# Attention's products in reverse order, a layer's weights through a ring of five buffers, and a bias added by an accumulating DMA

## The chip, the cores and the metric

The kernel runs on one core of a Trainium2 chip. A core has a matrix engine (TensorE, PE), a vector engine (VectorE, DVE), an activation engine (ScalarE, ACT), a general engine (GpSimd, POOL) and an engine that mostly issues transfers (SyncE, SP). Each of them executes its own list of instructions in the order in which it is written, and waits on semaphores for the others. Transfers run on 16 DMA engines, which serve several queues. In this kernel POOL issues the gathers (indirect DMAs) and some plain DMAs, all on one software queue, and SP issues most of the rest.

The metric is device time in microseconds (us) of one execution.

## The reference, cut to what matters

Two layers with the same outline, x = x + gnn(norm(x)) and then x = x + ffn(norm(x)), over x of 32 samples x 512 tokens x 256 features, with one adjacency matrix (512x512) for each sample.

Layer 0's ffn, for each token:

```python
t = max over d of (x[d] + Wt[f, d]) + bt[f]      # for each of 1024 features f
trop = s * max_i(t*sl_cvx + of_cvx) + (1-s) * min_i(t*sl_ccv + of_ccv)
classical = gelu(x @ Wc + bc);  g = sigmoid(x @ Wg + bg)
out = (g * trop + (1 - g) * classical) @ Wd + bd
```

`bd`, 256 numbers, is layer 0's last bias. Layer 1's gnn is attention with 4 heads of width 64 over the adjacency:

```python
h = einsum('bnd,hde->bhne', x, W)
weight = leaky_relu(e_src[i] + e_dst[j]), where adj == 0: -1e9
dst = einsum('bhij,bhje->bhie', softmax(weight), h) + bias
out = layernorm(relu(dst) + h) * gamma + beta
```

Layer 1's ffn assigns every token softly to 64 slices for each of 8 heads (`W_x`, `b_x`, `W_slice`, `b_slice`), gathers slice tokens (`W_fx`), runs a two-way state space scan with gates over the 64 slice tokens (`hy_in_w` of 1168x512, `hy_fcD_w` of 8x512, `hy_out_w` of 512x512), spreads the result back to the tokens and multiplies by `out_w` (256x512).

## The kernel before, in words

All is in float32. P is 128, the number of partitions; N is 512, the tokens of a sample; NT is 4, the tiles of 128 tokens in it; D is 256.

**Layer 0** (`layer0_sorted`). The gnn part (`convs`) goes over the samples in segments, normalises, and sorts the tokens of a segment by how many candidates their maximum over d needs. It writes a row for each token into a table in DRAM, `rows_of`, with its values and the indices of its largest entries. The ffn (`feed_forwards`) then works on 32 groups of 512 sorted tokens. Of a group:

- `sums` gathers the tokens' rows into `xs` (L553, four gathers of 128 rows on POOL), normalises each tile on ACT (`xn`, L574) and transposes it on PE. For each tile it gathers the table row of the largest entry (`best`, L564) and, one by one, those of the further entries (`rows`, L595); DVE takes the maximum into `best` (L598), after ACT added the value of the entry to its first row (L592). At its end come four adds on POOL, one for each tile, of the constant `bd` to `xs` (L610). `bd` is loaded at the start into all 128 partitions (L135 is the line of the helper that does it).
- `mixed` does the products with Wc and Wg (`clsp`, `gatep`, L623), transposes `best` (`tz`, L630), bends it (ACT L632 and L636, DVE L637) and blends (`acc`, up to L641).
- `down` multiplies by Wd (`po`, L652), adds into `xs` on DVE (L654), and stores `xs` to `x2s` in DRAM by a DMA of SP (L655).

`mixed` of a group is woven with `sums` of the next one; `down` of the group before comes after the first step of `mixed`. So the add of `bd` to a group's `xs` is written a whole group ahead of that group's `down`.

**The generator `ahead`**. Alongside, `feed_forwards` is woven with a second stream of steps, `ahead`: the convolutions of the later segments, and after these the beginning of layer 1 (`layer1_plain`). This beginning loads and transposes layer 1's weights, so their loading falls into layer 0's late groups, near 1850 to 2000 us. `load_T` (L995 to L1011) takes a weight in pieces of 128 rows: SP loads a piece into a buffer of the pool `raw` (L1005), PE transposes its blocks of 128 columns (L1009), ACT copies the result (L1010), and a step of the generator ends. W_fx has 4 pieces of 128x256, hy_in_w 9 of 128x512 and one of 16x512, hy_out_w 4, out_w 2 and hy_fcD_w one of 8x512: 21 in all. There are two buffers for each width of a piece. After them comes the block that forms the product of W_x and W_slice (`wsl`, up to L1075); it loads W_slice, W_x, b_x and b_slice itself, and squares `wsl` into a buffer `wsl2` (L1066).

**Layer 1** (`layer1_plain`). For each sample `prepare` gathers x, adds `ln_beta` by an accumulating DMA of POOL from a DRAM tile that holds the row four times (`add_rows`, L949), and makes the values `hv` and the terms of the weights. `attention` then goes over the four tiles j of 128 source tokens. Of each tile, DVE makes four weights `att`, one for each head, 128x512 each (L1220), in the order of the heads, some turns ahead; there are 13 buffers for them. When the last two heads' turn is there, PE makes all of the tile's products:

- eight `avp` products (L1256): two for each head, each with 32 columns of `hv` and the whole 128x512 weight. The output of the k-th goes to partitions 32k to 32k+31 of one of two PSUM tiles. So the four products of a PSUM tile use the four different groups of 32 columns of the array.
- four `adp` products (L1261), one for each head, for the sums that divide: again one for each column group.

The products of a tile are written in the order of the heads, so the first one takes the weight that was made first. The ffn (`mixer`) of two samples at a time is interleaved with the attention of later samples by a credit scheme. Its products are `lgp` L1342, `yTp` L1354, `xp` L1407, `gp` L1494, `segp` L1498, `xtp` L1503, `qp` L1508, `yp` L1524, `oTp` L1542, `outp` L1574; `hp` L1187 and `x3T` L1149 are of `prepare` of the next sample.

**Order**. The lines above are written by Python generators, and a scheduler then sets the order of each engine's list from what depends on what. The engines execute that list as it stands: an instruction that waits holds back what stands behind it on its engine.

Of the kernel before, what the change touches and what calls it, by code (L numbers as in the profile page):

```python
# [19 lines left out]
P = 128  # L20
# [77 lines left out]
def layer0_sorted(tc, ident, eps, x, adj, w, x2s, ranks, over, following):  # L98
# [29 lines left out]
    with ExitStack() as ctx:  # L128
# [9 lines left out]
        w_msg = const("w_msg", [P, DC, D], w["W_msg"].rearrange("(c p) u -> p c u", p=P))  # L138
        w_upd = const("w_upd", [P, DC, D], w["W_upd"].rearrange("(c p) u -> p c u", p=P))
        bias = const("bias", [P, D], w["bias"].partition_broadcast(P))  # L140
        bd = const("bd", [P, D], w["bd"].partition_broadcast(P))
        wc = cst.tile([P, DC, FFN], F32, tag="wc", name="wc")
        wg = cst.tile([P, DC, FFN], F32, tag="wg", name="wg")
        wd = cst.tile([P, FC, D], F32, tag="wd", name="wd")
# [398 lines left out]
        def feed_forwards():  # L543


            def sums(s, g):
# [57 lines left out]
                for c in range(DC):  # L604
# [1 line left out]
                nc.vector.tensor_tensor(over[:, s * ST : (s + 1) * ST].rearrange("p (t g) -> p g t", g=NG)[:, g, :],  # L606
                                        xg[:, :, COUNT], limits.rearrange("p (t g) -> p g t", g=NG)[:, g, :],
                                        ALU.is_gt)
                for t in range(NT):
                    nc.gpsimd.tensor_add(xg[:, t, :D], xg[:, t, :D], bd)  # L610
                got[s, g] = xg, xnT, best

            def mixed(s, g):
# [251 lines left out]
def layer1_plain(tc, ident, eps, x2s, ranks, adj, w, out, over, ps):  # L865
# [35 lines left out]
    with ExitStack() as ctx:  # L901
# [94 lines left out]

        with tc.tile_pool(name="raw", bufs=2, side="right") as raw:

            def load_T(dst, src, name):

                R, Ccols = src.shape
                for r0 in range(0, R, P):
                    n = min(P, R - r0)
                    t = raw.tile([P, Ccols], F32, tag=f"raw{Ccols}", name=f"{name}_{r0}")
                    nc.sync.dma_start(t[:n], src[r0 : r0 + n, :])  # L1005
                    pt = psum("tp", f"{name}p{r0}").rearrange("p (c r) -> p c r", r=P)
                    cs = Ccols // P
                    for c in range(cs):
                        nc.tensor.transpose(pt[:, c, :n], t[:n, c * P : (c + 1) * P], ident[:n, :n])  # L1009
                    nc.scalar.copy(dst[:, :, r0 : r0 + n], pt[:, :cs, :n])  # L1010
                    yield  # L1011

            yield from load_T(wfxT, w["W_fx"], "wfx")
            yield from load_T(inT, w["hy_in_w"], "in")
            yield from load_T(hoT, w["hy_out_w"], "ho")
            yield from load_T(owT, w["out_w"], "ow")
            yield from load_T(fcT, w["hy_fcD_w"], "fc")
# [5 lines left out]
            def twice_T(src, name):  # L1023

                R, Ccols = src.shape
                t = raw.tile([P, 2, Ccols], F32, tag="twice", name=name)
                for i in range(2):
                    nc.sync.dma_start(t[:R, i, :], src)
                pt = psum("tp", f"{name}p")
                nc.tensor.transpose(pt[:, :R], t[:R].rearrange("p i c -> p (i c)"), ident[:R, :R])  # L1030
                return pt


            wsT = raw.tile([P, G], F32, tag="wsT", name="wsT")
            nc.vector.tensor_copy(wsT, twice_T(w["W_slice"], "ws")[:, :G])
            wx = raw.tile([P, KC, D], F32, tag="wx", name="wx", bufs=1)
            nc.sync.dma_start(wx, w["W_x"].rearrange("(k p) d -> p k d", p=P))
            bx = raw.tile([P, KC], F32, tag="bx", name="bx")
            nc.sync.dma_start(bx, w["b_x"].rearrange("(k p) -> p k", p=P))
            bsl = raw.tile([1, H, G], F32, tag="bsl", name="bsl", bufs=1)  # L1040
            bs = raw.tile([1, G], F32, tag="bs", name="bs")
            nc.sync.dma_start(bs, w["b_slice"].rearrange("(o n) -> o n", o=1))
            for c in range(DC + 1):
                M = P if c < DC else 1
                for i in range(H // KC):

                    half = slice(i * C, (i + 1) * C)
                    px = psum("mm", f"wslp{c}_{i}")
                    for k in range(KC):
                        lhs = wx[half, k, c * P : (c + 1) * P] if c < DC else bx[half, k : k + 1]  # L1050
                        nc.tensor.matmul(px[:M, k * G : (k + 1) * G], lhs, wsT[half, :], start=True, stop=True)
                    px = px[:M, : KC * G].rearrange("p (k g) -> p k g", k=KC)
                    rt = rtemp[:M, i :: H // KC].unsqueeze(2).to_broadcast([M, KC, G])
                    if c < DC:
# [168 lines left out]
        def attention(b):  # L1223
# [21 lines left out]
            for i, (q, j) in enumerate(turns):  # L1245
# [4 lines left out]

                if q + 1 == AP:
                    ends = dict(start=j == 0, stop=j == NT - 1)
                    for p in range(AP):
                        for k in range(2 * HO // HW):
                            h, e = 2 * p + k * HW // HO, k * HW % HO
                            nc.tensor.matmul(pv[p][k * HW : (k + 1) * HW, :], hv[:, j, h, e : e + HW],  # L1256
                                             weighed[b, h, j], **ends)
                    if j == 0:
                        pd = psum("pv", f"adp{b}")
                    for h in range(AH):  # L1260
                        nc.tensor.matmul(pd[h * HW : (h + 1) * HW, :], hv[:, j, h, HO:].to_broadcast([P, HW]),  # L1261
                                         weighed.pop((b, h, j)), **ends)
                yield
# [983 lines left out]
```

## Time and profile before

| | |
|---|---|
| time, median of three runs | 4365.9 us (4364.42 to 4366.94) |
| profiled execution, its own time | 4372.35 us |
| span of the profiled execution | 4370.6 us |
| mean granted PE clock | 0.955 |
| PE busy | 3882.4 us, 89% |
| DVE busy | 3279.3 us, 75% |
| ACT busy | 2295.0 us, 53% |
| POOL busy | 1617.9 us, 37% |
| DMA, mean over the span | 116 GB/s |

The span is from the first to the last instruction. In the views that follow, a row of a stage names its stretch in us, then for each engine its busy time and its number of instructions; PEclk is the granted share of PE's full clock, and "DMA share" the mean busy share of the 16 DMA engines. A row "L1256 PE MATMUL avp<-att,hv 128*32 128x512 f32" reads: line 1256, on PE, a matmul with output `avp` from `att` and `hv`, with a stationary operand of 128x32 and a moving one of 128x512. In a row of waits, the first name is what stood and the second is what it stood for; the numbers are total us, times, and the longest. The chain of waits is followed backwards from the last instruction, at each step to what released it.

Layer 0's convolutions and groups fill the time up to about 2400 us, and layer 1's samples the time after it.

### The profile page before, as it was taken

The page shows a single profiled execution, that of the slowest core. Times are in us where ns is not written, and L with a number is a line of the kernel's source. Part 1 is how long each engine was busy: PE and PEld are TensorE (multiplying, and loading weights), DVE is VectorE, ACT ScalarE, POOL GpSimd, SP SyncE. Part 2 cuts the span into 40 slices and gives each one's busy share as a digit, 9 for nine tenths or more (in the row PEclk, how much of TensorE's full clock was granted, in tenths as well). Part 3 has the DMA queues.
Part 4 walks back from the last instruction along what each step waited for, and adds up shares of the span by engine and source line. Part 5 has one row for each costly group of instructions (what it writes and reads, how often), then busy time and mean ns, then how long its engine had stood idle before and what let it go on. Part 6 is the DMA issues. An engine that isn't in the chain of part 4 may idle for free.

```text
span 4370.6 us, 57973 instructions
## 1 busy us (share of the span) xinstructions
PE 3882.4 (89%) x20311; PEld 2456.1 (56%) x20311; DVE 3279.3 (75%) x7008; ACT 2295.0 (53%) x4756; POOL 1617.9 (37%) x2036
## 2 busy tenths in 40 slices
PE   5567898988989999888998899999999999999997
PEld 4454565565655666554555455655555555555555
DVE  6668887898878978877775777777777777777763
ACT  3345655566655656546564555555554455554533
POOL 2346644665536644354431322222222222222210
PEclk8778999999999999998999999999999999999998
DMA  5546543564436644375441322222222322222200
GB/s 128 160 154 216 179 156 126 165 218 143 153 117 199 199 156 135 93 250 167 147 133 40 95 73 73 69 65 72 68 68 76 78 75 78 64 74 77 61 25 21
DMA packets 244051, 507.52 MB, mean 116 GB/s; under 512 B 39299, under 2 KB 114827, under 8 KB 243748
## 3 DMA queue, kind: packets, MB, share of 16 engines
q0 software_dynamic: 107904, 349.50, 26.7%
q1 hardware_dynamic: 135844, 154.21, 11.3%
q8 instruction: 162, 2.65, 0.2%
q14 instruction: 141, 1.16, 0.1%
HBM read 446.46 MB, written 57.17 MB: 115 GB/s over the span
## 4 chain that ended last, share of the span: by engine, by line
DVE 33%; PE 32%; DMA 11%; issue 9%; POOL 8%; ACT 5%; SPq 0%; another core or an unknown queue 0%; DVEq 0%; POOLq 0%; ACTq 0%
DVE att L1220 4%; DVE acc L637 4%; PE clsp L623 4%; PE gatep L623 3%; PE po L652 3%; PE avp L1256 3%; DMA rows<-table,xs 2%; DVE best L598 2%; DMA rows<-table,tops 2%; DVE sw L1349 2%; DVE sst L1347 2%; PE yTp L1354 2%; DVE sw L1344 2%; PE oTp L1542 1%; DMA best<-table,xs 1%
## 5 line engine op out<-in xcount | busy, mean ns | idle before, releaser
L623 PE MATMUL clsp<-xnT,wc 128*128 128x512 f32 x1024 | 521.8, 628 | 55.5 <-ACT cls L625 39.7
L623 PE MATMUL gatep<-xnT,wg 128*128 128x512 f32 x1024 | 502.1, 609 | 10.5 <-ACT gate L625 9.7
L652 PE MATMUL po<-wd,acc 128*128 128x256 f32 x2048 | 456.9, 382 | 6.5 <-DVE acc L641 3.5
L652 PEld LDWEIGHTS po<-wd,acc 128*128 128x128 f32 x2048 | 388.8, 191 | 73.1 <-issue 9.2
L1220 DVE SCALAR_TENSOR_TENSOR att<-own,other,mask 128x512 f32<-128x512 f32 x512 | 366.1, 744 | 76.4 <-DMA own<-ownd 76.4
L637 DVE SCALAR_TENSOR_TENSOR acc<-past,fld,acc 128x512 f32<-128x512 f32 x448 | 346.3, 776 | 28.3 <-ACT past L636 20.3
L598 DVE SCALAR_TENSOR_TENSOR best<-rows,xs,best 128x1024 f32<-128x1024 f32 x212 | 273.1, 1290 | 121.4 <-ACT best L592 75.8
L632 ACT ACTIVATE acc<-tz,fld 128x512 f32<-128x512 f32 x256 | 199.0, 778 | 269.1 <-PE tz L630 237.5
L623 PEld LDWEIGHTS gatep<-xnT,wg 128*128 128x128 f32 x1024 | 197.3, 197 | 254.0 <-issue 200.8
L636 ACT ACTIVATE past<-tz,fld 128x512 f32<-128x512 f32 x448 | 291.6, 694 | 73.6 <-DVE acc L637 72.1
L595 POOL DMA_INDIRECT rows<-table,xs x212 | 247.3, 1166 | 176.7 <-DVE best L598 121.8
L1256 PE MATMUL avp<-att,hv 128*32 128x512 f32 x2048 | 297.4, 599 | 6.1 <-DVE att L1220 6.1
L623 PEld LDWEIGHTS clsp<-xnT,wc 128*128 128x128 f32 x1024 | 182.6, 199 | 195.2 <-issue 114.3
L434 PE MATMUL pm<-h,adj 128*128 128x258 f32 (+1 forms) x1024 | 178.9, 321 | 100.3 <-DVE keep L427 34.4
L625 ACT ACTIVATE gate<-gatep,fld 128x512 f32<-128x512 f32 x256 | 175.6, 686 | 153.4 <-PE gatep L623 130.4
L1342 PE MATMUL lgp<-wsl,x4T 128*128 128x512 f32 x512 | 241.4, 610 | 14.3 <-ACT sw L1343 6.7
L1354 PE MATMUL yTp<-sw,x 128*128 128x512 f32 x512 | 237.0, 602 | 17.4 <-DVE sw L1349 16.9
L1161 POOL DMA_INDIRECT x<-x2s,ranks x128 | 135.2, 1056 | 295.5 <-DVE att L1220 147.5
L553 POOL DMA_INDIRECT xs<-rows_of,order x128 | 158.8, 1241 | 229.7 <-DVE acc L637 111.8
L1307 POOL TENSOR_TENSOR mu<-mu,eps 128x16 f32<-128x16 f32 x32 | 111.3, 3478 | 350.4 <-DVE mu L1306 350.4
L1574 PE MATMUL outp<-v,swT 128*128 128x256 f32 x1024 | 227.6, 381 | 0.0
L625 ACT ACTIVATE cls<-clsp,fld 128x512 f32<-128x512 f32 x256 | 176.3, 689 | 94.4 <-PE clsp L623 59.1
(598 smaller groups left out, 8809.0 us busy)
## 6 DMA issues: line engine op xcount, KB each, us to landing
adj<-in_adj POOLq DMA_DIRECT2D x128, 256.0 KB
ai<-in_adj SPq DMA_DIRECT2D x128, 256.0 KB
x<-added POOLq DMA_DIRECT2D x64, 512.0 KB
own<-ownd SPq DMA_DIRECT2D x128, 256.0 KB
rows_of<-keep SPq DMA_DIRECT2D x32, 550.0 KB
x<-in_x SPq DMA_DIRECT2D x32, 512.0 KB
x2s<-xs SPq DMA_DIRECT2D x32, 512.0 KB
out<-x SPq DMA_DIRECT2D x32, 512.0 KB
```

Source lines behind the costliest of these rows:

```text
L595: nc.gpsimd.indirect_dma_start(out=row, out_offset=None, in_=table, in_offset=bass.IndirectOffsetOnAxis(ap=idxs[:, k : k + 1].bitcast(U32) ...
L598: nc.vector.scalar_tensor_tensor(m, row, vals[:, k : k + 1], m, ALU.add, ALU.max)
L623: nc.tensor.matmul(pf, wf[:, c, f * P : (f + 1) * P], xnT[:, c, :], start=c == 0, stop=c == DC - 1)
L625: nc.scalar.activation(o, pf, fn, bias=fld[:, f, bf : bf + 1], scale=1.0 if fn == AF.Gelu else 0.5)
L636: nc.scalar.activation(r, z, AF.Relu, bias=fld[:, f, AT + b : AT + b + 1])
L637: nc.vector.scalar_tensor_tensor(y, r, fld[:, f, CH + b : CH + b + 1], y, ALU.mult, ALU.add)
L652: nc.tensor.matmul(po[:, i, :], acc[f][:, t * P : (t + 1) * P], wd[:, f, :], start=f == 0, stop=f == FC - 1)
L1220: nc.vector.scalar_tensor_tensor(e, own[h], other[:, j, h : h + 1], mask[:, j, :], ALU.max, ALU.mult)
L1256: nc.tensor.matmul(pv[p][k * HW : (k + 1) * HW, :], hv[:, j, h, e : e + HW], weighed[b, h, j], **ends)
L1342: nc.tensor.matmul(pf, xnT[:, c, t * P : (t + 1) * P], wsl[:, c, :], start=c == 0, stop=c == DC - 1)
L1354: nc.tensor.matmul(py, xn[:, t, c * P : (c + 1) * P], sw[:, t, :], start=t == 0, stop=t == NT - 1)
L1574: nc.tensor.matmul(po[:, :D], swT[:, k, t * P : (t + 1) * P], v[:, k, :], start=k == 0, stop=k == KC - 1)
```

## The change

Three edits.

1. **`bd` by an accumulating DMA.** The constant in 128 partitions and its load go. A DRAM tile of four rows is filled with the 256 numbers four times. For each group, in the place of the four adds on POOL, one DMA issued by POOL adds this tile, broadcast to all partitions, to the first 256 columns of the four rows of `xs` in each partition.
2. **Layer 1's weights through one ring.** W_x, W_slice (twice), b_x and b_slice are loaded first. The 21 pieces of the five other weights form one list and share five buffers of one shape. Three pieces are asked for before a step of the generator ends; then each step asks for the piece three on and transposes its own. `wsl2` takes two of the same buffers, in place of its own.
3. **The products in reverse.** The loops over the PSUM tiles and column groups of `avp`, and over the heads of `adp`, run backwards: the first product takes the weight made last.

```diff
-        bd = const("bd", [P, D], w["bd"].partition_broadcast(P))
...
+        bd = dr.tile([NT, D], F32, tag="bd", name="bd", bufs=1)
+        nc.sync.dma_start(bd, w["bd"].partition_broadcast(NT))
...
-                for t in range(NT):
-                    nc.gpsimd.tensor_add(xg[:, t, :D], xg[:, t, :D], bd)
+                nc.gpsimd.dma_start(xg[:, :, :D], bd.partition_broadcast(P), accum_op=ALU.add)
...
-            def load_T(dst, src, name):
-                R, Ccols = src.shape
-                for r0 in range(0, R, P):
-                    n = min(P, R - r0)
-                    t = raw.tile([P, Ccols], F32, tag=f"raw{Ccols}", name=f"{name}_{r0}")
-                    nc.sync.dma_start(t[:n], src[r0 : r0 + n, :])
...
-            yield from load_T(wfxT, w["W_fx"], "wfx")
-            yield from load_T(inT, w["hy_in_w"], "in")
...
+            wx = raw.tile([P, KC, D], F32, tag="wx", name="wx", bufs=1)
+            nc.sync.dma_start(wx, w["W_x"].rearrange("(k p) d -> p k d", p=P))
+            twice = raw.tile([P, 2, w["W_slice"].shape[1]], F32, tag="twice", name="ws", bufs=1)
+            for i in range(2):
+                nc.sync.dma_start(twice[:G, i, :], w["W_slice"])
...
+            def fetch(i):
+                _, src, r0 = pieces[i]
+                n = min(P, src.shape[0] - r0)
+                t = raw.tile([P, DI], F32, tag="piece", name=f"piece{i}", bufs=5)
+                nc.sync.dma_start(t[:n, : src.shape[1]], src[r0 : r0 + n, :])
+                return t
+            coming = [fetch(i) for i in range(3)]
+            yield
+            for i, (dst, src, r0) in enumerate(pieces):
+                if i + 3 < len(pieces):
+                    coming.append(fetch(i + 3))
...
-                sq = raw.tile([P, H * G], F32, tag="wsl2", name=f"wsl2_{c}")
+                sq = raw.tile([P, H * G], F32, tag="piece", name=f"wsl2_{c}", bufs=5)
...
-                    for p in range(AP):
-                        for k in range(2 * HO // HW):
+                    for p in reversed(range(AP)):
+                        for k in reversed(range(2 * HO // HW)):
...
-                    for h in range(AH):
+                    for h in reversed(range(AH)):
```

More of the change, by code (lines that the diff above doesn't have):

```diff
@@ L997, in layer1_plain @@
         with tc.tile_pool(name="raw", bufs=2, side="right") as raw:
-            def load_T(dst, src, name):
-                R, Ccols = src.shape
-                for r0 in range(0, R, P):
-                    n = min(P, R - r0)
-                    t = raw.tile([P, Ccols], F32, tag=f"raw{Ccols}", name=f"{name}_{r0}")
-                    nc.sync.dma_start(t[:n], src[r0 : r0 + n, :])
[L1006 to L1011, printed above, removed]
@@ L1013, in layer1_plain @@
-            yield from load_T(wfxT, w["W_fx"], "wfx")
-            yield from load_T(inT, w["hy_in_w"], "in")
-            yield from load_T(hoT, w["hy_out_w"], "ho")
-            yield from load_T(owT, w["out_w"], "ow")
-            yield from load_T(fcT, w["hy_fcD_w"], "fc")
+            wx = raw.tile([P, KC, D], F32, tag="wx", name="wx", bufs=1)
+            nc.sync.dma_start(wx, w["W_x"].rearrange("(k p) d -> p k d", p=P))
+            twice = raw.tile([P, 2, w["W_slice"].shape[1]], F32, tag="twice", name="ws", bufs=1)
@@ new lines, in layer1_plain @@
+            for i in range(2):
+                nc.sync.dma_start(twice[:G, i, :], w["W_slice"])
+            bx = raw.tile([P, KC], F32, tag="bx", name="bx")
+            nc.sync.dma_start(bx, w["b_x"].rearrange("(k p) -> p k", p=P))
+            bs = raw.tile([1, G], F32, tag="bs", name="bs")
+            nc.sync.dma_start(bs, w["b_slice"].rearrange("(o n) -> o n", o=1))
+            pieces = [(dst, w[name], r0)
+                      for dst, name in ((wfxT, "W_fx"), (inT, "hy_in_w"), (hoT, "hy_out_w"), (owT, "out_w"),
+                                        (fcT, "hy_fcD_w"))
+                      for r0 in range(0, w[name].shape[0], P)]
@@ new lines, in fetch @@
+            def fetch(i):
[9 more added lines that the diff above has]
+                    coming.append(fetch(i + 3))
+                n, cs = min(P, src.shape[0] - r0), src.shape[1] // P
+                pt = psum("tp", f"piecep{i}").rearrange("p (c r) -> p c r", r=P)
+                for c in range(cs):
+                    nc.tensor.transpose(pt[:, c, :n], coming[i][:n, c * P : (c + 1) * P], ident[:n, :n])
+                nc.scalar.copy(dst[:, :, r0 : r0 + n], pt[:, :cs, :n])
+                yield
@@ L1021, in layer1_plain @@
                 nc.vector.tensor_scalar_mul(hoT[:, c, :], hoT[:, c, :], norm[:, c : c + 1])
[L1023 to L1031, printed above, removed]
-            wsT = raw.tile([P, G], F32, tag="wsT", name="wsT")
[L1035 to L1039, printed above, removed]
+            pt = psum("tp", "wsp")
+            nc.tensor.transpose(pt[:, :G], twice[:G].rearrange("p i c -> p (i c)"), ident[:G, :G])
+            wsT = raw.tile([P, G], F32, tag="wsT", name="wsT")
+            nc.vector.tensor_copy(wsT, pt[:, :G])
             bsl = raw.tile([1, H, G], F32, tag="bsl", name="bsl", bufs=1)
-            bs = raw.tile([1, G], F32, tag="bs", name="bs")
-            nc.sync.dma_start(bs, w["b_slice"].rearrange("(o n) -> o n", o=1))
             for c in range(DC + 1):
```

## The prediction

> **What bounds the kernel now.** I read the busy time by stage first, because the three edits lie in three stages.
>
> ```profile
> core 0: us, PE busy (x) PEld busy (x) DVE busy (x) ACT busy (x) POOL busy (x), PEclk, DMA share, GB/s
> 350.00:1850.00 1500.00, 1340.91 (x5366) 878.12 (x5365) 1245.81 (x2479) 872.17 (x1494) 800.85 (x1058) 0.96 0.50 162
> 1850.00:2000.00 150.00, 125.74 (x470) 77.41 (x469) 111.28 (x163) 78.75 (x127) 78.89 (x68) 0.88 0.66 219
> 2000.00:2390.00 390.00, 363.19 (x1288) 219.76 (x1286) 280.68 (x372) 231.60 (x367) 125.28 (x117) 0.97 0.36 118
> ...
> 2480.00:4200.00 1720.00, 1645.69 (x11064) 992.49 (x11063) 1277.97 (x2864) 882.41 (x2271) 429.27 (x391) 1.00 0.26 70
> ```
>
> The last row is layer 1 in its steady state. PE is busy for 1645.69 of 1720 us, 95.7%, and DVE for 74%: PE time saved there is kernel time, nearly one for one. The first row is layer 0. PE has 89%, DVE 83%, and nobody leads, so the chain of waits decides. Summed by line over 350 to 2390 us it holds 275 us of landing gathers (rows, best, xs), and only 13.6 us of the POOL adds of L610. The second row is the stretch in which layer 1's weights are loaded; the DMA engines are at their fullest, 0.66, and PE at its emptiest, 84%.
>
> Then the timeline of PE, for a steady group of layer 1 (whole array blocks, then a broken one):
>
> ```profile
> 3011.12 1.92 PE L1256 MATMUL avp<-att,hv 128*32 128x512 f32 x16
> 3012.86 1.04 PE L1261 MATMUL adp<-att,hv 128*32 128x512 f32 x8
> 3013.72 1.02 PE L1256 MATMUL avp<-att,hv 128*32 128x512 f32 x2
> 3014.67 3.84 PE L1407 MATMUL xp<-uT,inT 128*128 128x128 f32 x32
> ...
> 3036.05 1.49 PE L1256 MATMUL avp<-att,hv 128*32 128x512 f32 x11
> ...
> 3037.90 2.05 PE L1187 MATMUL hp<-wa,x3T 128*128 128x264 f32 x8
> 3039.88 1.06 PE L1261 MATMUL adp<-att,hv 128*32 128x512 f32 x6
> 3040.87 1.90 PE L1524 MATMUL yp<-xk,mix 64*64 64x64 f32 x32
> ```
>
> A product is two records. Eight products (x16) take 1.74 us to the next start and four more (x8) 0.86: four run side by side, 0.86 us for four. But one alone (x2) takes 0.95 us before xp starts. And the three adp after hp take 0.99.
>
> Last the views of the bias and of the weights' transposes:
>
> ```profile
> L610 POOL TENSOR_TENSOR xs<-xs,bd x128: 625/730/1775, 301.7 to 2313.9; 128x256 f32<-128x256 f32 x128
> ...
> its engine sat idle before it (us, times) until:
>   ACT xn L574: 164.8, 39
> ```
>
> ```profile
> L949 POOL DMA_DIRECT2D x<-added x64: 856/914/1041, 2404.4 to 4280.5; - x64
> ```
>
> ```profile
> PE inp L1009 <- DMA in<-in_L_ffn_hy_in_w: 7.4, 4, 3.4
> PE wfxp L1009 <- DMA wfx<-in_L_ffn_W_fx: 4.1, 1, 4.1
> PE hop L1009 <- DMA ho<-in_L_ffn_hy_out_w: 3.2, 1, 3.2
> ```
>
> 128 adds of 0.73 us median; 64 accumulating DMAs that layer 1 already has, 0.91 us of POOL each; and PE standing 14.7 us for weights that had not landed.
>
> **What the Trainium skill says.** TensorEngine Tiling (Array Packing), Key Properties: tiles run independently of each other, and a change of tiling mode drains the array. The trace agrees on the first (four products in 0.86 us, each record about 0.6 long); the drain is at most the 0.09 us by which the lone product exceeds a slot. DMA: Bandwidth & Descriptors, SWDGE vs HWDGE vs iDMA: only GpSimd can issue an accumulating DMA, and its software queue has one context. So the new DMA stands in line with the gathers of the table; the trace has layer 1's accumulations and all gathers on queue 0. GPSIMD Engine Reference, Elementwise — side-by-side cycle accounting: 2.6 cycles an element for a two-input add, an estimate of 0.55 us for 256 elements at 1.2 GHz plus dispatch; the trace has 0.73, which I use.
>
> **The attention's order.** No product is added or removed. What changes is where PE's written order breaks. In the order before, PE's schedule takes one avp product early, when the first weight of a token tile is there, goes to other work (xp, or gp and what follows), and returns for the other seven. It also parts the four adp as one, hp, three, 15 times. In the order after, the early piece is a whole group of four, with all four columns filled, and adp stays together. Counted over the whole program, with each unbroken run priced by its fullest column, the runs need 401 slots before and 385 after (384 is the floor, 128 blocks of three). 16 slots x 0.86 = 13.8 us. The quoted group by its starts: before 0.95 + 5.29 (3026.72 to 3032.01) + 1.85 (3036.05 to 3037.90) + 0.99 = 9.08 us; after 0.90 + 6 slots 5.16 + 2 slots 1.74 = 7.80. That is 1.3 us, in about 15 groups 19 us. I take 16 us. A wait is also moved: the block now begins with the weight made last, so everything behind it on PE (gp, segp, xtp, qp, and through them DVE's dq and mix) waits for it. In this group DVE ends its last weight at 3030.6 and PE would want it at about 3031.5, 0.9 us of slack. DVE's and ACT's own orders in layer 1 stay all but the same (some 20 of DVE's 6840 instructions move there or near). Bounds: from -19 us to +15, the latter if the slack is missing in all of the 15 groups by the 2.2 us of three weights (0.74 each), 33 us, less the gain. Buffers of att come free in reverse, up to 2 us later for the next one wanted; DVE has no wait for them now, and 13 buffers stand against 4 in a block.
>
> **The ring of weights.** 21 pieces and 21 groups of transposes stay, and PE's work with them. Before, two buffers of a kind; SP waited 63.2 us in L1005 for transposes. After, five, with three asked for ahead, and W_x, W_slice (twice), b_x and b_slice issued first. Those are five issues of about 0.5 us on SP, 2.6 us in all, and 512 KB in front of the first piece. So I expect the first transposes, which PE reaches at 1864.6, to stand about 2 us; the 4.1 us stand at 1868 goes, as all four W_fx pieces are out before it. The nine hy_in pieces no longer come two at a time: five lie ready when PE reaches them at about 1920. But PE's order now packs 14 pieces between clsp of one group and gatep of the next, with little else between; pieces 9 to 17, 2.3 MB, must come in that time, and at the 321 GB/s that this trace reached between 1920 and 1940 that is 7 us and a landing of 5 to 7. PE's own work there is 14 x 0.43 + 8 halves x 0.86 = 13 us. I leave 6 of the 10.6 us of stands there. Sum: 14.7 - 2 - 6 = 7 us less waiting; the chain after 1890 runs through gathers, POOL and DVE rather than these stands, so I count 5. Bounds -12 to +6. SP's x2s store is queued between pieces; nobody waits for it soon. The second weight block (wsl) moves back by a few us and layer 1 does not need it before 2470.
>
> **The bias.** Removed: 128 x 0.73 = 93 us of POOL; added: 32 issues x 0.91 = 29 us. POOL is 53% busy there, so only what lies on the chain counts: 13.6 us, less 32 x 0.91 x (13.6/110, the share of the adds' 110 us busy that is on the chain) = 3.6: 10 us won. The new DMA waits for ACT's xn of the fourth tile, and the gathers of rows and best stand behind it on POOL, as they stood behind the fourth add: no change. On the DMA engines: the trace has layer 1's accumulation as 128 packets of 4 KB of about 340 ns, against 159 for a gather's; 128 x 340/16 = 2.7 us of all engines. Layer 0's has the same bytes with rows of 1 KB at the destination; it may cost more, and the trace of before does not show one. 32 x 2.7 = 87 us raises the DMA share from 0.50 by 0.04. In the order after, about half of the 32 are followed at once by gathers, issued 1.25 us apart; the first of them comes 2.7 - 1.25 = 1.5 us late, and so do those behind it until there is slack. At most 32 x 1.5 = 48 us; with half followed by gathers and less than half of those on the chain, 10 us. Sum 0; bounds -14 (no harm) to +38. The store of x2s needs the add to have landed, but down() comes a whole group later. The buffer of bd (1 KB) is freed, for nothing.
>
> **Sum.** -16 - 5 + 0 = -21 us. The profiled execution took 4372.35 us with 4370.6 in its span, so 4351 by its clock; it lies 6.4 us over the median 4365.9, and the prediction for the median is 4345 us. 0.2%, 8.7 us, is about what a measurement of this kernel can tell from no change.
>
> **Rivals.** (1) Slower: the accumulation holds the gathers' queue. If its 1 KB rows make it 5 us instead of 2.7, or all 32 hit gathers that DVE is waiting for, it costs 32 x 1.5 or more; it decides from (21 + 10)/32 = 1.0 us of critical delay per group on. With 1.7 us: +54 - 31 = +23, 4389. For it: 275 us of gathers on the chain. Against it: layer 0's end (2000 to 2390) is PE's, at 93%. (2) No change: each aligned piece waits for its last weight by about the 1.1 us that it saves, and the weights' stands just move to the pack: 4362. For it: DVE is on the chain of layer 1 with 10.2% in att; against it, the 0.9 us of slack. (3) Much faster: POOL is what spaces the gathers in layer 0, and its 64 us freed and some of the 164.8 us of waiting for xn return a third: another 25 us, 4320. Against it: 13.6 us on the chain.
>
> **Chances.** Main case 0.50 (4330 to 4357), rival 3 0.12, rival 2 0.14, rival 1 0.24. Faster 0.62, same 0.14, slower 0.24. The range leaves out the far end of rival 3 and of rival 1: 4322 to 4388.
>
> **What would show it.** Right: in the timeline of layer 1 no avp x2 alone and no adp x6 after hp; busy time of PE for 2480 to 4200 with one or two per cent less per group; no wait of L1256 above some 20 us. POOL in layer 0 some 60 us less busy, the new DMA 32 times, about 128 packets each. Wrong: idle of PE before avp or gp released by att; rows, best or xs landing later in the chain by more than 30 us in sum; PE standing over 15 us for pieces.

## The result

The changed kernel takes 4322.07 us (median of six runs, 4316.0 to 4332.06); the kernel before, measured beside it, 4365.16 us. The ratio is 0.9906 with a 95% interval of 0.989 to 0.9923: 43 us faster, by the interval 33 to 48. The direction was the predicted one, and the size was twice the 21 us that the sum had. The profiled execution took 4319.15 us, with a span of 4317.4.

The same stages of the profile of after, with the columns of the first view of before (stretch, busy time of each engine with its instructions, granted PE clock, DMA share, GB/s):

```profile
350.00:1850.00 1500.00, 1362.06 (x5432) 893.43 (x5431) 1228.59 (x2511) 882.09 (x1512) 749.56 (x995) 0.96 0.56 172
1850.00:2000.00 150.00, 128.16 (x536) 79.31 (x535) 120.40 (x166) 88.69 (x153) 77.48 (x64) 0.97 0.76 251
...
2480.00:4200.00 1720.00, 1637.87 (x11189) 1004.20 (x11188) 1273.29 (x2874) 882.15 (x2247) 432.70 (x396) 1.00 0.26 69
```

In layer 0's 1500 us PE now does more (x5432 against x5366), and DVE does more instructions (x2511 against x2479) in less busy time (1228.59 against 1245.81 us). POOL has 51 us less. In layer 1's 1720 us PE runs 125 records more in 8 us less, and the other engines changed little. The lead of after over before, read from the start of the first `clsp` product of each group and the first `avp` product of each sample in the two traces, says where the time went:

| start of | before | after | lead, us |
|---|---|---|---|
| group 8 of layer 0 | 876.5 | 859.8 | 17 |
| group 16 | 1409.4 | 1389.6 | 20 |
| group 24 | 1930.7 | 1908.0 | 23 |
| group 25 | 2017.4 | 1972.7 | 45 |
| group 31, the last | 2328.9 | 2279.8 | 49 |
| sample 0 of layer 1 | 2422.1 | 2377.2 | 45 |
| sample 31 | 4196.3 | 4141.6 | 55 |

Some 20 us come in the first half of layer 0, where only the bias differs; 22 in the one group in which the weights are loaded; 10 in layer 1, after a loss of 4 at its entry. These are single executions, in which 8 us of lead can arise by chance, as the second edit alone will show. (The spans differ by 53 us, since the profiled execution of before lay above its median and that of after below.)

The steps that the prediction named can be seen. The bias, on POOL, by its line (count: shortest/median/longest ns, first and last start):

```profile
L610 POOL DMA_DIRECT2D xs<-bd x32: 1322/1408/1476, 319.3 to 2264.9; - x32
```

32 DMAs, 1.41 us of POOL each, where 0.91 was taken from layer 1's; 45 us in place of 110. PE's waits for the weights' pieces, in the stretch from 1790 to 2350 us (us in total, times, longest):

```profile
PE piecep L1031 <- DMA piece<-in_L_ffn_hy_out_w: 3.4, 3, 1.9
...
PE piecep L1031 <- DMA piece<-in_L_ffn_hy_in_w: 1.9, 3, 1.0
...
PE piecep L1031 <- DMA piece<-in_L_ffn_out_w: 0.5, 1, 0.5
```

5.8 us stand where 14.7 stood. And the timeline of the group of layer 1 that was quoted of before:

```profile
2965.64 1.92 PE L1258 MATMUL avp<-att,hv 128*32 128x512 f32 x16
2967.38 1.04 PE L1263 MATMUL adp<-att,hv 128*32 128x512 f32 x8
2968.24 1.04 PE L1258 MATMUL avp<-att,hv 128*32 128x512 f32 x8
2969.21 3.84 PE L1409 MATMUL xp<-uT,inT 128*128 128x128 f32 x32
...
2990.59 1.06 PE L1258 MATMUL avp<-att,hv 128*32 128x512 f32 x8
2991.48 1.04 PE L1263 MATMUL adp<-att,hv 128*32 128x512 f32 x8
2992.45 2.05 PE L1188 MATMUL hp<-wa,x3T 128*128 128x264 f32 x8
```

The piece before `xp` is four products (x8) in 0.97 us where one had taken 0.95, and `adp` is no longer parted by `hp`.

What no step of the prediction had is in the line of DVE's `acc`, first of before, then of after:

```profile
L637 DVE SCALAR_TENSOR_TENSOR acc<-past,fld,acc x448: 711/745/2194, 322.2 to 2367.4; 128x512 f32<-128x512 f32 x150
```

```profile
L637 DVE SCALAR_TENSOR_TENSOR acc<-past,fld,acc x448: 710/745/801, 317.9 to 2318.2; 128x512 f32<-128x512 f32 x150
```

The same 448 instructions have the same median, and the long ones are gone: the longest went from 2194 to 801 ns. They lay beside the adds of the bias. From before's timeline, two of them:

```profile
1053.51 1.49 DVE L637 SCALAR_TENSOR_TENSOR acc<-past,fld,acc 128x512 f32<-128x512 f32 x1
1053.79 0.66 POOL L610 TENSOR_TENSOR xs<-xs,bd 128x256 f32<-128x256 f32 x1
...
1055.53 0.74 DVE L637 SCALAR_TENSOR_TENSOR acc<-past,fld,acc 128x512 f32<-128x512 f32 x1
```

```profile
954.50 0.63 POOL L610 TENSOR_TENSOR xs<-xs,bd 128x256 f32<-128x256 f32 x1
954.55 0.60 DVE L450 SCALAR_TENSOR_TENSOR shiftb<-mv,rsb 128x4 f32<-128x4 f32 x1 [1.63 <-POOL rsb L31]
...
955.07 0.68 DVE L408 TENSOR_TENSOR h<-ph,h 128x512 fp32r<-128x512 f32 x1
```

An instruction of 0.74 us takes 1.49, longer by about the add of 0.66 that began within it; and one on 128x4 elements ends with the add, after 0.60 us, where its median is 0.16. To count this, each DVE instruction of the first 2400 us was compared with the median of its line and shape, and the excess put to the POOL instruction that it overlapped most. In before the excess beside L610 is 39.5 us, and all the rest together 1.2; in after all of it is -1.5.

The Trainium skill says this in SBUF — State Buffer, Who interferes with whom: "A DVE instruction with two SBUF inputs contends with a GpSimd instruction that reads SBUF", not with one that only writes. The prediction had not used that page. Before's trace agrees. Beside the adds, 16 instructions that read one of their two inputs from PSUM (the memory that PE's products go to; L408, L427, L439, L654) were over their medians by -0.06 us in 4.15 us of overlap, and 23 with one input (`sta` L40, `stb` L445) by 0.05 us in 7.4. The excess lies on those that read two inputs from SBUF: L637 has 14 us of it, the other `acc` lines 18, `best` 7. Whether this is worth 40 us of the kernel, or POOL's time itself is, had to be tried.

### The profile page after: what moved, and what is told of

It is laid out like the page before. It is cut to its first block, busy times and chain, and to the rows that moved or that the text cites. A ratio compares the mean times of both kernels' runs of the same rounds, so it can differ in the third digit from the quotient of the medians.

```text
span 4317.4 us, 57903 instructions
## 1 busy us (share of the span) xinstructions
PE 3852.3 (89%) x20311; PEld 2446.7 (57%) x20311; DVE 3233.1 (75%) x7008; ACT 2290.3 (53%) x4756; POOL 1540.2 (36%) x1940
## 4 chain that ended last, share of the span: by engine, by line
PE 35%; DVE 26%; DMA 10%; issue 9%; POOL 8%; ACT 5%; SPq 0%; POOLq 0%; DVEq 0%; ACTq 0%
PE clsp L623 5%; DVE att L1221 4%; PE gatep L623 4%; PE po L652 3%; PE avp L1258 3%; DVE acc L637 3%; DMA rows<-table,xs 2%; PE yTp L1356 2%; DVE best L599 2%; DMA best<-table,xs 2%; DVE sw L1351 2%; DMA rows<-table,tops 2%; DVE sst L1349 2%; DVE sw L1346 2%; PE oTp L1544 1%
## 5 line engine op out<-in xcount | busy, mean ns | idle before, releaser
L637 DVE SCALAR_TENSOR_TENSOR acc<-past,fld,acc 128x512 f32<-128x512 f32 x448 | 332.1, 744 | 32.5 <-ACT past L636 24.3
L1258 PE MATMUL avp<-att,hv 128*32 128x512 f32 x2048 | 254.9, 603 | 13.9 <-DVE att L1221 13.8
L435 PEld LDWEIGHTS pm<-h,adj 128*128 128x128 f32 x1024 | 152.5, 214 | 123.9 <-issue 73.0
```

The lines of the kernel that those rows point to most:

```text
L435: nc.tensor.matmul(pm[:, : c1 - c0], a[:, i, t * P : (t + 1) * P], h[:, i, c0:c1], start=i + c0 == 0, stop=i + 1 == NT and c0 > 0)
L637: nc.vector.scalar_tensor_tensor(y, r, fld[:, f, CH + b : CH + b + 1], y, ALU.mult, ALU.add)
```

## The experiments

Theory A: the adds cost by stretching DVE. Theory B, close to the prediction and its third rival: the adds cost POOL's time, on the chain or ahead of the gathers. For the ring and the order: what was counted of PE's stands and runs, against other waits. Times are medians in us, and a gain in us is the difference of the medians; a ratio, with its 95% interval, is to the kernel before in the same comparison. It is taken from all runs and can differ from the ratio of the medians by some 3 us' worth.

### Each edit alone

```diff
-                for t in range(NT):
-                    nc.gpsimd.tensor_add(xg[:, t, :D], xg[:, t, :D], bd)
+                nc.gpsimd.dma_start(xg[:, :, :D], bd.partition_broadcast(P), accum_op=ALU.add)
```

> Edit 1 alone: bd by the accumulating DMA. Theory A (the trace of before has VectorE's instructions 39.5 us over their medians in layer 0 while they overlap the adds of L610, and 1.2 us over beside everything else): VectorE gets about 40 us back, and since it is on the chain for about half of layer 0, the kernel is about 20 us faster (15 to 28). Theory B (the prediction's): only the 13.6 us of adds on the chain count, and the DMA's landing takes them back: within 6 us of before. Theory C: the gain seen in layer 0 comes from the other two edits through the scheduler's order: within 6 us as well, with the last group of layer 0 no earlier.

Measured: 4338.59 against 4367.32, 0.9934 [0.992, 0.9948]: 29 us faster. That is theory A's size, just above its range. The prediction had 0 for this edit.

The second edit, the whole ring as in the change, alone:

> Edit 2 alone: the ring of five buffers. Theory A (between 1930 and 2017 us VectorE stood 11.8 us for the scaling of hoT, waiting for ScalarE's last copy of hy_out_w, and the gathers of rows stood 11.9 us behind VectorE): about 20 us faster (12 to 25), nearly all of it between the starts of groups 24 and 25 of layer 0, where before takes 87 us. Theory B (the prediction's sum: 14.7 us of TensorE's stands, less new ones): 5 us faster, not more than 8.

Measured: 4358.49 against 4367.32, 0.9973 [0.9957, 0.9988]: 9 us faster by the medians, 12 by the ratio, 5 to 19 by its interval. This lies between the two theories. In its trace the lead goes from 3 to 25 us between groups 24 and 25, and 17 are left at group 31: some of the gain is given back in the next group. (8 us of lead stand at group 16 already, ahead of anything that this edit touches: so much can a single execution differ.)

The third, the reversed loops alone:

> Edit 3 alone: the products in reverse. The prediction has 16 us less, spread over layer 1 with about 1.3 us in each pair of samples that had a lone product. In the trace of after, the lead over before grows by 8 to 10 us from the first to the last product of layer 1. So: 8 to 10 us faster if the broken runs cost less than was counted or a new wait takes some; 16 us if the other edits hide the rest; 0 if the growth was the clock's.

Measured: 4359.58 against 4367.32, 0.998 [0.997, 0.9989]: 8 us faster (5 to 13). In the trace, from the first `xp` to the last `outp`, PE's time in unbroken runs of `avp` and `adp`, each from its start to the next other start and without the waits, fell from 324.8 to 309.7 us: 15.1, against the 16 of the prediction. PE's idle time there rose from 93.5 to 97.5, and the stretch as a whole is 11.5 us shorter. Ahead of it lies a loss. From the timeline of this kernel:

```profile
2422.74 0.28 PE L1200 MATMUL minep<-ident,mine 128*16 128x128 f32 x1 [0.45 <-ACT hv L1191]
2422.85 0.61 PE L1091 MATMUL maskp<-identb,a 128*128 128x128 bf16 x8
2428.07 3.64 PE L1256 MATMUL avp<-att,hv 128*32 128x512 f32 x16 [4.61 <-DVE att L1220]
```

At sample 0 nothing else is ready, and the reversed block stands 4.61 us for its last weight, where the old order began at 2422.06 with what was there. So layer 1 starts 6 us later, and 8 by the first `xp`. In this trace some 3 us are left of the 11.5; over all runs the medians have 8.

The bias left out altogether (the two lines of the adds removed, nothing in their place, so this kernel does not add `bd`):

> The bias bd is left out of layer 0 altogether: no adds, no DMA. It is the ceiling of edit 1. If the accumulating DMA costs the gathers nothing, as fast as edit 1 alone, within 4 us. If it holds the gathers' queue by 1.5 us in a third of the groups, as the prediction has it, 10 us or more faster than edit 1 alone.

Measured: 4324.27 against 4367.32, 0.99 [0.9884, 0.9917]: 43 us faster than before, 14 faster than edit 1. The order of the instructions hardly differs from before's: when the two traces are laid side by side, 45 of 7008 instructions on DVE stand elsewhere, 19 of 1908 on POOL, and 65 of PE's 8134 records ahead of layer 1. So the 43 us come from the adds' absence, not from another order. The three edits alone sum to 28.7 + 8.8 + 7.7 = 45 us by the medians (49 by the ratios); together they gave 43 (41). The intervals don't part the sum from the whole.

### What the adds cost

POOL as busy as before, in the same places, but without reading:

```diff
                 for t in range(NT):
-                    nc.gpsimd.tensor_add(xg[:, t, :D], xg[:, t, :D], bd)
+                    for _ in range(3):
+                        nc.gpsimd.memset(xg[:, t, :D], 0.0)
```

> Before with each of the 128 adds replaced by three GpSimd writes of zeros over the same 128x256 (so layer 0's ffn block leaves out its residual x and bd; the time counts, not the output). GpSimd is busy about as long as with an add, at the same place, behind the same wait for xn, but reads nothing. Theory A (GpSimd's reads stretch VectorE's two-input instructions): VectorE's excess over its medians beside L610 falls from 39.5 to below 5 us, and the kernel is 25 to 43 us faster than before, near the kernel without the bias. Theory B (GpSimd's time and its waits in order count): within 10 us of before.

Measured: 4331.91 against 4365.36, 0.9929 [0.9909, 0.9949]: 33 us faster. The groups of before (busy, mean ns, idle before and what ended it), then those of this kernel's page:

```profile
L637 DVE SCALAR_TENSOR_TENSOR acc<-past,fld,acc 128x512 f32<-128x512 f32 x448 | 346.3, 776 | 28.3 <-ACT past L636 20.3 <-DVE shifta L46 0.3
...
L610 POOL TENSOR_TENSOR xs<-xs,bd 128x256 f32<-128x256 f32 x128 | 109.3, 859 | 165.9 <-ACT xn L574 164.8
```

```profile
L638 DVE SCALAR_TENSOR_TENSOR acc<-past,fld,acc 128x512 f32<-128x512 f32 x448 | 332.5, 744 | 31.4 <-ACT past L637 23.6
...
L611 POOL MEMSET xs<- 128x256 f32 x384 | 118.9, 317 | 163.8 <-ACT xn L574 151.6 <-ACT xnT L605 0.8 <-issue 0.6
```

POOL spends 118.9 us there, more than the adds' 109.3, and stands 151.6 us for `xn`, as before (164.8). Yet `acc` has a mean of 744 ns in place of 776, as in the changed kernel, and the excess beside L611 is -0.5 us. The order is close to before's again (91 of 7008 DVE instructions stand elsewhere). Theory B falls as the main cause, and so the reading is worth some 33 us. To POOL's time and waits are left at most the 10 us by which this kernel lies behind the one without the bias, and the intervals of these two overlap.

The dose doubled:

```diff
                     nc.gpsimd.tensor_add(xg[:, t, :D], xg[:, t, :D], bd)
+                    nc.gpsimd.tensor_add(xg[:, t, :D], xg[:, t, :D], bd)
```

> Before with every add of bd on GpSimd made twice (bd is zeros in this data, so the sum is unchanged). Theory A (reads on GpSimd stretch VectorE): VectorE's excess beside L610 and L611 rises from 39.5 to about 80 us, and the kernel is 30 to 45 us slower. If only the adds on the chain count: 14 us slower or less.

Measured: 4419.16 against 4373.78, 1.0111 [1.0094, 1.0127]: 45 us slower. The excess beside the two adds is 75.1 us, against 39.5, and with all the rest 81.4, against 40.7. From its groups:

```profile
L638 DVE SCALAR_TENSOR_TENSOR acc<-past,fld,acc 128x512 f32<-128x512 f32 x448 | 358.0, 802 | 22.9 <-ACT past L637 15.2
```

So 0, 40 and 75 us of stretching beside the adds go with -43, 0 and +45 us of the kernel. These steps change POOL's own time too. Where POOL's time was kept and only its reading left out, 33 us went with the 39.5: an estimate, from these two numbers, of 0.8 us of kernel time for each us of stretching.

The add on DVE itself:

```diff
-                for t in range(NT):
-                    nc.gpsimd.tensor_add(xg[:, t, :D], xg[:, t, :D], bd)
+                nc.vector.tensor_add(xg[:, :, :D], xg[:, :, :D], bd.unsqueeze(1).to_broadcast([P, NT, D]))
```

> Before with the four adds of bd on GpSimd replaced by one add of 128x1024 on VectorE for each group. GpSimd is freed of 110 us, as with no bias at all; VectorE gets 32 instructions of about 1.3 us (best, of 128x1024 with two inputs, takes 1.28), 42 us, and is spared the 39.5 us of stretching. Theory A (sharing: what counts is VectorE's time): within 10 us of before, where leaving the bias out gives 43 less. Theory B (GpSimd's time or its waits for xn in front of the gathers count): 25 us or more below before.

Measured: 4334.97 against 4365.36, 0.9931 [0.9916, 0.9946]: 30 us faster, where theory A's bookkeeping said within 10. The instruction takes 1.22 us, 39 us in all, about what the stretching took, but costs the kernel only 43 - 30 = 13. DVE's microseconds are not all alike, then. What differs: with an instruction of its own the scheduler set another order, while the stretching hits `acc` and `best` in an order that does not reckon with it. In the traces some 610 of 7008 DVE instructions stand elsewhere than before, and some 2300 of PE's 8134 records ahead of layer 1. That this is the reason was argued, not shown.

### The ring

DVE stood 11.8 us for the scaling of `hoT` in the group of the weights. From the waits of before, 1930 to 1990 us:

```profile
POOL rows L595 <- DVE best L598: 18.3, 7, 11.3
DVE hoT L1021 <- ACT hoT L1010: 11.8, 1, 11.8
ACT inT L1010 <- PE inp L1009: 11.7, 5, 5.6
...
PE inp L1009 <- DMA in<-in_L_ffn_hy_in_w: 5.1, 2, 3.4
```

Read upwards: PE stands for pieces, ACT for PE, DVE for ACT, and the gathers of `rows` for DVE. To take DVE's stand away alone, the scaling was tied to a later value:

```diff
-            for c in range(KC):
-                nc.vector.tensor_scalar_mul(hoT[:, c, :], hoT[:, c, :], norm[:, c : c + 1])
...
             nc.scalar.activation(ebsl, ebsl, AF.Exp)
+            nc.vector.scalar_tensor_tensor(norm, most[:, 0:1].to_broadcast([P, KC]), 0.0, norm, ALU.mult, ALU.add)
+            for c in range(KC):
+                nc.vector.tensor_scalar_mul(hoT[:, c, :], hoT[:, c, :], norm[:, c : c + 1])
```

> Before with its two buffers of a kind and its loads; only the scaling of hoT by norm (four VectorE instructions) is tied to a value made some 25 us later, so that VectorE no longer stands for ScalarE's last copy of hy_out_w. Theory A (the stand of 11.8 us on VectorE, with the gathers behind it, is what the ring takes away): group 25 starts 12 to 22 us earlier than before, and the kernel is 8 to 16 us faster, as with the ring. Theory B (the ring's earlier landings and TensorE's stands count): within 4 us of before.

Measured: 4367.88 against 4365.36, 1.0004 [0.9993, 1.0014]: nothing that can be told. Group 25 starts 5.6 us earlier in its trace, not 12 to 22. In its timeline DVE stands in the same stretch for the next ones behind the late pieces, and not for `hoT`:

```profile
1957.33 1.28 DVE L598 SCALAR_TENSOR_TENSOR best<-rows,tops,best 128x1024 f32<-128x1024 f32 x1 [9.43 <-ACT best L592]
1962.62 0.69 DVE L654 TENSOR_TENSOR xs<-xs,po 128x512 f32<-128x512 f32 x1 [4.01 <-PE po L652]
```

So the theory that this one stand was the ring's gain falls. The buffers alone, without the asking ahead, the extra step and the early loads:

```diff
-                    t = raw.tile([P, Ccols], F32, tag=f"raw{Ccols}", name=f"{name}_{r0}")
-                    nc.sync.dma_start(t[:n], src[r0 : r0 + n, :])
+                    t = raw.tile([P, DI], F32, tag="piece", name=f"{name}_{r0}", bufs=5)
+                    nc.sync.dma_start(t[:n, :Ccols], src[r0 : r0 + n, :])
...
-                sq = raw.tile([P, H * G], F32, tag="wsl2", name=f"wsl2_{c}")
+                sq = raw.tile([P, H * G], F32, tag="piece", name=f"wsl2_{c}", bufs=5)
```

> Before with nothing of edit 2 but the buffers: the pieces of all five weights share five buffers of one shape (wsl2 two of them); the loop asks for a piece and transposes it in the same step as before, and W_x, W_slice, b_x and b_slice stay where they are. If earlier landings of hy_in_w and hy_out_w are what the ring brings: group 25 starts 15 to 22 us earlier than before and the kernel is 8 to 14 us faster, like edit 2 alone (12). If the asking three ahead, the extra step or the loads put first matter: within 5 us of before.

Measured: 4359.33 against 4373.78, 0.997 [0.9956, 0.9985]: 14 us faster (7 to 19), as much as the whole second edit within the intervals. Its trace gains 20 us between the starts of groups 24 and 25, where the whole edit's has 22. So the five buffers are enough for the gain; a few us of the rest can't be excluded. DVE's stand for `hoT` is gone from the trace, and PE stands 3.2 us for pieces of hy_out_w and out_w.

### The order's loss at the entry

```diff
-                    for p in reversed(range(AP)):
-                        for k in reversed(range(2 * HO // HW)):
+                    for p in range(AP)[:: -1 if b else 1]:
+                        for k in range(2 * HO // HW)[:: -1 if b else 1]:
...
-                    for h in reversed(range(AH)):
+                    for h in range(AH)[:: -1 if b else 1]:
```

> After, but sample 0 of layer 1 keeps the old order of its products; all others are reversed. In the trace of after, TensorE waits 13.4 us for weights in the first two samples (before: 5.4), and the lead over before falls by 4 us between the last group of layer 0 and sample 0. If the reversed block's wait for its last weight, with no other work ready, is that loss: about 4 us faster than after (2 to 6). If it comes from elsewhere: the same as after within 2 us.

Measured: 4327.74 against 4373.78, 0.9899 [0.9882, 0.9916], which can't be told from after's 0.9906; 4 us are less than these intervals resolve. In the trace sample 0 loses 1 us of the lead in place of 4, but by sample 4 another 3 are gone: PE's waits for `att` near the entry are 12.0 us, against 13.4. The wait moved to the next reversed blocks.

### What the accumulating DMA costs

After, with the DMA written later, away from the next group's gathers:

```diff
-                nc.gpsimd.dma_start(xg[:, :, :D], bd.partition_broadcast(P), accum_op=ALU.add)
...
                     nc.vector.scalar_tensor_tensor(y, y, 0.5, out["cls"], ALU.mult, ALU.add)
+                    if f == 4:
+                        nc.gpsimd.dma_start(xg[:, :, :D], bd.partition_broadcast(P), accum_op=ALU.add)
```

> After with the accumulating DMA of a group moved from the end of sums to behind the fifth of the eight steps of mixed, away from the gathers of the next group's first rows. If the DMA's cost (14 us between leaving the bias out and edit 1) comes from GpSimd and its queue being taken just where the next gathers are due, this is 5 to 14 us faster than after. If the cost is its share of the DMA engines or of GpSimd's time wherever it stands, within 4 us of after.

Measured: 4326.8 against 4365.36, 0.9908 [0.9893, 0.9923]: no different from after. But this edit did not move the DMA. The scheduler set POOL's order from what depends on what, and in the trace 29 of the 32 DMAs stand at the same place among POOL's instructions as in after. All but two start within 2 us of the same distance from their group's first `clsp`, most of them some 15 us ahead of it. So whether its place is what it costs was not tested.

The bias over TensorE, with sample 0 as before:

```diff
-                nc.gpsimd.dma_start(xg[:, :, :D], bd.partition_broadcast(P), accum_op=ALU.add)
...
+                        nc.tensor.matmul(po[:, i, :], ones.to_broadcast([P, P]), bd3, start=True, stop=False)
                         for f in range(FC):
                             nc.tensor.matmul(po[:, i, :], acc[f][:, t * P : (t + 1) * P], wd[:, f, :],
-                                             start=f == 0, stop=f == FC - 1)
+                                             start=False, stop=f == FC - 1)
```

> As e9_first_as_before, but bd goes neither over GpSimd nor by a DMA: TensorE adds it into po by one more product for each of the 128 tiles (bd split into three bfloat16 parts in three rows of a 128x256 operand, with ones as the other), some 0.11 to 0.15 us each, 14 to 19 us of TensorE in all, about half of it on the chain. If the accumulating DMA costs 14 us and the products cost 7 to 10, this is 3 to 8 us faster than e9 and the fastest of all. If the DMA's cost was the noise of two medians: slower than e9 by 5 or more.

Measured: 4322.09 against 4373.78, 0.9883 [0.9868, 0.9899]: 6 us below the kernel with sample 0 in the old order and the DMA (4327.74), with overlapping intervals. Then the four ways of the bias on top of the other two edits, in one comparison (before: 4368.95):

> After itself, beside the three that follow: 0.9906 of before, 41 us faster (33 to 48).

> After with the bias bd left out of layer 0: no DMA, no add. The accumulating DMA's cost on top of the other two edits. If it is what edit 1 alone showed: 14 us faster than after (8 to 18). If the two medians deceived and the traces were right: 5 us or less.

> After with bd added by one more TensorE product for each of the 128 tiles instead of the DMA (35 us of busy TensorE in the trace of its like, some 20 us of its time without overlap). If the DMA costs 14: 4 to 9 us faster than after. If the DMA costs 5: 3 to 10 us slower.

> After with bd added by one VectorE instruction of 1.22 us for each of the 32 groups instead of the DMA, 39 us of VectorE in all. On top of before this was 30 us faster, where the DMA was 29 us faster: within 5 us of after.

| bias | median | ratio to before |
|---|---|---|
| by the DMA (after) | 4326.12 | 0.9905 [0.989, 0.9921] |
| left out | 4312.86 | 0.9879 [0.9862, 0.9897] |
| on TensorE | 4321.99 | 0.9895 [0.9877, 0.9912] |
| on VectorE | 4325.35 | 0.9903 [0.9886, 0.9921] |

The DMA costs 13 us, as it did on top of before (14). VectorE costs the same, and TensorE 4 less, which these runs don't resolve. None of the ways that add the bias beats the changed kernel by more than the measurement can tell. What of the DMA costs stays open: its share of the 16 engines (0.56 with it, 0.52 without any bias, from 350 to 1850 us), POOL's 1.41 us, or its place. A stretching of DVE it is not: all the excess of after is -1.5 us.

## Why the prediction was wrong

**The bias: the gain was mis-sized.** The failed sentence is "POOL is 53% busy there, so only what lies on the chain counts: 13.6 us". The adds were costed by their own time, and what they did to DVE, which is no edge of the chain of waits and no idle time, was put at nothing. It could be read from before: L637 has a mean of 776 ns over a median of 745, L598 of up to 1319 over 1282, and the longest `acc` was three times the median. The adds themselves had a mean of 859 ns over a median of 730, which is why 128 x 0.73 gave 93 us in the prediction where they were busy for 110. In place of 10 us won the runs have 43 with the bias left out, of which some 33 come with the reads alone (the writes of zeros). The other half of the term, 10 us lost to the new DMA, measured 13 to 14. So 0 became 29.

**The DMA's details.** Taken as 128 packets of 4 KB, it moved 16896 more packets on its queue, 528 for each of 32 DMAs; 512 of them are of 1 KB, and at 106 ns each in the mean they take 3.4 us of all engines, where 2.7 was priced. It landed after 5.7 us in the median. In after's trace the next gather started within 3 us in only 8 of the 32 cases, and 13 us later in the median. The gathers of rows, best and xs on the chain from 350 to 2390 us are 262 us before (the prediction's 275 had 12.6 us of loads of x among them) and 268 after: rival 1, which needed more than 1 us of critical delay in each group beyond the gains, did not come.

**The ring: mis-sized.** The 14.7 us of PE's stands less 8 were near the right size (5.8 remain), but "the chain after 1890 runs through gathers, POOL and DVE rather than these stands, so I count 5" took the links for separate ones. By the view of waits, POOL stood there for DVE, DVE for ACT, and ACT for PE and the pieces. The runs have 9 us by the medians and 12 by the ratio, with 22 in the trace's one group and part given back; 5 is at the edge of the interval. That the buffers bring it is shown; by which of these waits is not.

**The order: right in the run, too large in the sum.** 15.1 us of PE's time in the products against 16 counted. In the quoted group the products take 8.12 us by their starts (0.97, 5.29 from 2981.26 to 2986.55, 1.86), not the 7.80 of the prediction, against 9.08 before. A full piece before `xp` takes 0.97, 0.11 over a slot of 0.86, where the prediction called 0.09 the most for the drain. The wait that was priced as a bound came at the entry, 4.6 us at sample 0, and PE's other waits took 4 more. 8 us measured.

**The sum** -16 - 5 + 0 = -21 should have been -7.7 - 8.8 - 28.7 = -45 by the edits alone, and is -43 together. Rival 3 named 4320, near what came, but not by its mechanism: POOL's 64 us freed. With POOL as busy as ever and only its reads gone, 33 us came.

## What to carry to other kernels

An engine that is off the chain can still cost the kernel time, by making another engine's instructions longer: here 33 us for 39.5 of stretching. So compare the mean and the longest of a line with its median, and ask what runs beside the long ones: here adds on GpSimd that read SBUF stretched VectorE's two-input instructions. Where several engines stand in one stretch, follow each wait to its source before the stands are weighed apart; removing the nearest one moves the wait to the next. And where a scheduler sets the order, look in the trace whether an edit that moves an instruction has moved it.

## What the runs showed of the hardware that was not expected

- A GpSimd add of 128x256 beside VectorE instructions with two inputs lengthened those that read both from SBUF by 39.5 us in 128 adds, 0.31 us an add; even one of 128x4 elements took 0.60 us in place of 0.16. Those with one input in PSUM were not lengthened (-0.06 us in 16). GpSimd writes of the same 128x256, 0.31 us each, lengthened nothing (-0.5 us in 384).
- An accumulating DMA with four 1 KB rows in each partition took GpSimd 1.41 us to issue, against 0.91 for layer 1's with 4 KB in one piece.
